# Layer 0's sixth inner product and layer 1's own block sums in a two-layer graph network

## The chip, the core and the metric

The kernel runs on one core of a Trainium2 chip, in one launch. The metric is the device time of that launch in microseconds (us). Before the change it is 2325.86, the median of three runs (2325.35 to 2327.71).

## The reference, cut to what matters

Sixteen batches of N = 1024 nodes with D = 512 features, in float32, share one symmetric 1024 x 1024 adjacency matrix. Two layers follow one another; `layernorm` works over the features.

```python
# layer 0
h = maximum(layernorm(x), 0)
x = x + (einsum('nm,bmd->bnd', adj, h) @ W0 + bias)
# layer 1: graph attention
u  = maximum(layernorm(x), 0)
h  = u @ W1                              # (b, 1024, 512)
s1, s2 = h @ a[:512], h @ a[512:]
e  = leaky_relu(s1[:, :, None] + s2[:, None, :], 0.2) * adj
x  = x + elu(einsum('bij,bjf->bif', softmax(e, axis=2), h) + beta * h)
```

In layer 0 the left matrix of the large product is the same for all batches. In layer 1 it is the batch's own attention matrix.

## The kernel before, in words

**Two phases.** Layer 0 runs for all sixteen batches, then layer 1 for all sixteen. Between them, each batch's residual x1 and its u lie in DRAM. The core's memory is divided into pools of tiles; those that matter here are `b4` (twelve tiles of 512 KB: 128 partitions x 1024 float32), `up` (seven of that size), `xp` (four, residuals), `ld` (two, loads) and `b2` (five of half the size). The eight banks of the matmul engine's result memory (PSUM) are taken from a pool of eight.

**Seven products instead of eight.** Each large product is cut into 2 x 2 blocks and made by the Strassen-Winograd scheme with seven block products, `p1` to `p7` (`PRODUCTS`, L44 to L52). Left operands are the blocks A11, A12, A22 and the sums S1 = A21 + A22, S2 = S1 - A11, S3 = A11 - A21, S4 = A12 - S2; right operands the blocks B11, B21, B22 and the sums T1 = B12 - B11, T2 = B22 - T1, T3 = B22 - B12, T4 = B21 - T2. The order on the matmul engine is p1, p2, p6, p5, p7, p3, p4. Each product has two halves of 128 x 512 results, one PSUM bank each; products that share a letter in `PRODUCTS` accumulate in the same pair of banks (p1, p6, p7 and p4 in Y, p5 and p3 in X, p2 alone in W).

**Reading the banks.** `ReadA` (L121 to L174) takes each finished half out of its bank: p1, p6, p5 and p4 by a copy on ScalarE (to C11, C12, C22, C21), p2 and p7 by an addition on VectorE onto such a copy, p3 by three or four VectorE additions, which make the left operands of the second product. Names in the profile follow: `y` is layer 0's product with the adjacency, `po` its product with W0, `z` layer 1's product with the attention matrix, `pq` its product with W1.

**The inner level.** In layer 0, from the second batch on (`products_a2`, L198 to L311), four of the seven block products, p1, p5, p3 and p4, are cut once more, into seven inner products r1 to r7 of 256-column matmuls (`inner_steps`, L206); p2, p6 and p7 are plain products of eight 512-column matmuls. An inner product needs:

- left sums, three of them and one in place, made per batch on VectorE by `inner_left` (L393), in a tile of `b4`;
- right sums, three of them and one in place, made once in the first batch by `inner_right` (L368) and kept for all of layer 0, in `up`, `b4` and `b2` tiles;
- a scratch tile `t` of `b4`, and combinations: copies on ScalarE after r1, r5 and r7, additions on VectorE after r6, r7 and r3.

The three pairs (p1, p2), (p5, p6), (p3, p7) go in turns: one inner step, one plain step. p4 goes in turns with the first product with the weights.

**Order of the work.** Every engine executes its instructions in the order in which the code issues them (`InOrder`, L103 to L115). The code of a product calls `after(k)` behind each of its steps, and plans map a step k to the helpers that are called there. So the plans decide what stands ahead of what in each engine's queue. In `products_a2` a step is one turn: 0 to 6 for (p1, p2), 7 to 13 for (p5, p6), 14 to 20 for (p3, p7), 21 to 27 for p4. In layer 1, `layer1_a` (L854) has fourteen steps, two per product: step 2n + p is half p of the n-th product, after its bank has been read. `layer1_b` (L869) has fourteen in the same manner for the weighted products.

**What the plans place in layer 0.** `plan_out` (L1083) makes layer 1's u of the *previous* batch from its residual tiles, in place: `stats` (two passes of ScalarE per 128 rows, then the inverse deviation on GpSimd), `relu` (ScalarE), `logits` (VectorE, two reductions per 128 rows, for s1 and s2), `sums` (VectorE, the block sums S1, S2, S4 of u, S3 in place) and `store` (SyncE issues seven stores: four blocks of u, and S1, S2, S4). It also loads the next residual (`load_res`, L548) and calls `inner_left`. The unwanted full result of a `stats` or `logits` pass goes into the tile of S1, which is written later.

**What the plans place in layer 1.** `load_u` (L693) loads the seven tiles of the next batch's u, at the steps in `LOADS_U` (L1170). The softmax of the next batch (`Softmax`, L714) is spread over both parts by `SOFTMAX_A` and `SOFTMAX_B`: row maxima on VectorE, exponentials on ScalarE, transposes on VectorE. Its right sums are made on VectorE: T1 and T2 in the part with W1 (steps 1, 2, 5, 6), T3 at its steps 12 and 13, T4 at steps 6 and 8 of the next batch's `layer1_a`:

```python
SOFTMAX_B = {0: "D", 1: "T1a", 2: "T1b", 4: "d", 5: "T2a", 6: "T2b", 12: "T3a", 13: "T3b"}
LATE_A = {6: "T4a", 8: "T4b"}
```

The u of the last batch is not ready in layer 0. `LateOut` (L663) makes it in pieces during layer 1, and its block sums are made from the loaded blocks by `u_sums` (L701), at steps 10 and 12 of `layer1_b`.

All rows of the profile carry line L111, that of the helper that records each instruction; instructions are told apart by their tiles.

## Time and profile before

| | |
|---|---|
| median of three runs | 2325.86 us |
| the profiled execution: time | 2330.04 us |
| its span (first to last instruction) | 2328.3 us, 28484 instructions |
| matmul engine (PE) busy | 2292.2 us, 98% |
| VectorE (DVE) | 1808.8 us, 78% |
| ScalarE (ACT) | 1503.0 us, 65% |
| GpSimd (POOL) | 586.5 us, 25% |
| DMA | 383.15 MB, mean 165 GB/s |
| clock granted to the matmul engine | 0.996 |
| layer 0, first batch with the set-up | 0 to 89.8 us |
| layer 0, batches 1 to 15 | 89.8 to 1151.9 us |
| layer 1 | 1151.9 us to the end |

Busy time is the sum of an engine's instructions, waits left out. The names of tiles in a row stand as output<-inputs, with numbers of batches left out. Times in a timeline are counted from the start of the span. A bracket at the end of a row gives the idle time before it in us and the instruction whose end closed it.

### The profile page before, as it was taken

What the parts mean: (1) busy time and instruction counts of PE and PEld (TensorE: products, weight loads), DVE (VectorE), ACT (ScalarE), POOL (GpSimd) and SP (SyncE); (2) the same over time, 40 slices, a digit from 0 to 9 for tenths busy, and PEclk for the clock granted to TensorE, in tenths of its full rate; (3) what the DMA queues carried; (4) which work ended last, traced back from release to release, by engine and by line L of the source; (5) the groups of instructions that cost most, each with busy time, mean ns of one, the idle gap of its engine ahead of it and who ended that gap; (6) DMA issues with size and microseconds to landing.
All of it is one profiled execution on the core that took longest, in us unless ns stands there. A gap on an engine that the chain in (4) does not pass through costs nothing.

```text
span 2328.3 us, 28484 instructions
## 1 busy us (share of the span) xinstructions
PE 2292.2 (98%) x7984; PEld 1511.3 (65%) x7984; DVE 1808.8 (78%) x3932; ACT 1503.0 (65%) x4025; POOL 586.5 (25%) x680
## 2 busy tenths in 40 slices
PE   9999999999999999999899999999999999999998
PEld 5777777777777777776655566555665556655565
DVE  7687787888787788787787778777877778777774
ACT  3666667666667566766357667677676776667743
POOL 1333323233323333222101222122220222112220
PEclk9999999999999999999999999999999999999999
DMA  6255443455453455443755546655466554565541
GB/s 212 82 190 179 157 159 129 141 191 182 145 170 114 152 190 164 145 150 108 268 170 164 177 160 200 199 169 193 160 194 197 172 173 151 176 194 156 179 128 42
DMA packets 207247, 383.15 MB, mean 165 GB/s; under 512 B 80240, under 2 KB 88432, under 8 KB 207088
## 3 DMA queue, kind: packets, MB, share of 16 engines
q1 hardware_dynamic: 206768, 380.81, 50.0%
q8 instruction: 63, 1.03, 0.2%
q14 instruction: 96, 0.79, 0.1%
q10 hardware_dynamic: 320, 0.52, 0.1%
HBM read 251.92 MB, written 133.50 MB: 166 GB/s over the span
## 4 chain that ended last, share of the span: by engine, by line
PE 41%; DVE 18%; ACT 17%; DMA 15%; issue 4%; SPq 3%; POOL 3%; DVEq 0%; ACTq 0%; POOLq 0%
PE z_Y L111 8%; PE y_Y L111 6%; PE pq_Y L111 4%; ACT e L111 4%; ACT uS L111 4%; PE po_Y L111 4%; PE z_X L111 4%; DVE e L111 3%; DMA md<-mx 3%; SPq L111 3%; DVE uS L111 3%; DMA x<-in_x_dram 3%; PE z_W L111 2%; DMA mask<-maskd 2%; PE pq_X L111 2%
## 5 line engine op out<-in xcount | busy, mean ns | idle before, releaser
L111 POOL TENSOR_TENSOR x<-x,r 128x512 f32<-128x512 f32 x120 | 226.1, 1895 | 883.8 <-DMA ul_S<-ud_S 398.7
L111 ACT ACTIVATE e<-e,nm 128x256 f32<-128x256 f32 x480 | 237.4, 498 | 168.3 <-DVE nm L111 168.3
L111 DVE CUSTOM_DVE_ANT_0 e<-e,mask 128x256 f32<-128x256 f32 x512 | 239.2, 519 | 73.1 <-DMA mask<-maskd 42.9
L111 POOL TENSOR_TENSOR xr<-xr,bias_bc 128x512 f32<-128x512 f32 x128 | 172.8, 1362 | 231.1 <-DVE xr L111 164.4
L111 PE MATMUL z_Y<-pT,ul_U 128*128 128x512 f32 x512 | 224.9, 592 | 0.0
L111 ACT ACTIVATE e<-s2b,s1b 128x256 f32<-128x256 f32 x512 | 215.1, 507 | 9.2 <-DMA s2b<-s2d 9.2
L111 DVE STREAM_TRANSPOSE pT<-e 128x512 f32<-128x512 f32 x240 | 155.7, 687 | 67.3 <-ACT e L111 67.3
L111 DVE CUSTOM_DVE_ANT_0 uS<-xr,v_bc 128x512 f32<-128x512 f32 x240 | 165.3, 689 | 54.0 <-ACT uS L111 49.4
L111 PE MATMUL po_Y<-w_c,y_C 128*128 128x256 f32 x768 | 192.1, 385 | 7.5 <-DVE xr L111 7.4
L111 PE MATMUL pq_Y<-w_c,z_C 128*128 128x256 f32 x768 | 176.4, 381 | 2.2 <-ACT z L111 1.0
L111 PEld LDWEIGHTS z_Y<-pT,ul_U 128*128 128x128 f32 x512 | 97.3, 190 | 115.6 <-issue 112.2
L111 ACT ACTIVATE r<-z,rs 128x256 f32<-128x256 f32 x192 | 95.7, 499 | 112.1 <-DVE z L111 112.1
L111 PEld LDWEIGHTS po_Y<-w_c,y_C 128*128 128x128 f32 x768 | 147.8, 193 | 30.4 <-DVE xr L111 9.3
L111 PEld LDWEIGHTS pq_Y<-w_c,z_C 128*128 128x128 f32 x768 | 144.6, 190 | 33.4 <-issue 7.7
L111 PE MATMUL y_Y<-adjT_B,h 128*128 128x512 f32 (+1 forms) x332 | 149.7, 554 | 1.4 <-ACT adjT_B L111 1.4
L111 ACT ACTIVATE h<-x,nb_h,r_h 128x512 f32<-128x512 f32 (+1 forms) x132 | 98.1, 792 | 73.8 <-POOL nb_h L111 73.2
L111 ACT ACTIVATE uS<-xr 128x512 f32<-128x512 f32 x120 | 75.4, 629 | 85.2 <-DVE xr L111 65.1
L111 PE MATMUL y_Y<-adjT_T,hS 128*128 128x512 f32 x256 | 128.0, 596 | 0.0
L111 PE MATMUL y_W<-adjT_B,h 128*128 128x512 f32 x256 | 127.2, 592 | 0.0
L111 PE MATMUL po_X<-w_c,y_S 128*128 128x256 f32 x512 | 115.7, 379 | 0.0
L111 PE MATMUL pq_X<-w_c,z_S 128*128 128x256 f32 x512 | 115.6, 379 | 0.0
L111 PE MATMUL z_W<-pT,ul_U 128*128 128x512 f32 x256 | 112.5, 592 | 0.0
(202 smaller groups left out, 4891.3 us busy)
## 6 DMA issues: line engine op xcount, KB each, us to landing
mask<-maskd SPq DMA_DIRECT2D x128, 512.0 KB
x<-in_x_dram SPq DMA_DIRECT2D x64, 512.0 KB
xr<-in_x_dram SPq DMA_DIRECT2D x256, 128.0 KB
x1d<-xr SPq DMA_DIRECT2D x64, 512.0 KB
ul_U<-ud_U SPq DMA_DIRECT2D x64, 512.0 KB
x<-x1d SPq DMA_DIRECT2D x64, 512.0 KB
out_dram<-x SPq DMA_DIRECT2D x252, 128.0 KB
ud_U<-xr SPq DMA_DIRECT2D x60, 512.0 KB
```

The source lines that it names most:

```text
L111: return lambda *args, **kwargs: tc.keep_in_program_order(f(*args, **kwargs))
```

## The change

It has two parts, and a rearrangement around them.

**Inner products.** p2 and p6 become inner products too, so six of seven are. The pairs (p1, p2) and (p5, p6) are now two inner products in turns: r1 of one, r1 of the other, r4, r4, and so on. Where p6 was read in the middle and at the end of its pair, it is now read at the last two turns, beside p5. p3 with p7 and p4 with the weights stay as they were. `INNER` has six entries, the right sums take eight tiles instead of five (seven of `up`, one of `b4`) and the same two of `b2`; `plan_first` makes those of p2 and p6 in the first batch, and `plan_out` and `plan_norm_b` call `inner_left` for p2 and p6 in each.

**Sums of u.** Layer 0 stores only the four blocks of u, each right after its `relu`; `LayerOut.sums` and the three stores of S1, S2, S4 go. Layer 1 loads four blocks and makes the sums with `u_sums`, now in two parts: S1 and S2 (part 0) at steps 10 and 12 of the previous batch's `layer1_b`, S3 and S4 (part 1) at steps 3 and 4 of the batch's own `layer1_a`. For batch 0, part 0 stands at steps -1 and 0 of `layer1_a`. Since the S1 tile that took the unwanted results is no more, there is a tile `junk` of `b4`, which is kept.

**Rearrangement.** `plan_out` has a new order of statistics, normalisations, logits and loads of residuals. In layer 1, T3 moves from steps 12 and 13 of `layer1_b` to steps 5 and 6 of `layer1_a`, and T4 from steps 6 and 8 to 9 and 11.

```diff
-        for two, one in (("p1", "p2"), ("p5", "p6"), ("p3", "p7")):
-            inn, pla = inner_steps(two), plain_steps(one)
-            for m in range(7):
-                inn[m]()
-                pla[m if m < 4 else m + 1]()
-                if m == 0 and two == "p5":
+        for pair in (("p1", "p2"), ("p5", "p6")):
+            turns = list(zip(*(inner_steps(prod) for prod in pair)))
+            for m, turn in enumerate(turns):
+                for step in turn:
+                    step()
+                if m == 0 and k:
                     reads("p2", 0)
                     reads("p2", 1)
-                elif m == 3:
-                    pla[4]()
-                    if one != "p2":
-                        reads(one, 0)
-                elif m == 5:
-                    reads(two, 0)
-                elif m == 6:
-                    for prod in (two,) if one == "p2" else (one, two):
-                        reads(prod, 1)
+                elif m > 4:
+                    for prod in pair:
+                        if prod != "p2":
+                            reads(prod, m - 5)
                 after(k + m)
             k += 7
+        inn, pla = inner_steps("p3"), plain_steps("p7")
+        for m in range(7):
+            inn[m]()
+            pla[m if m < 4 else m + 1]()
+            if m == 3:
+                pla[4]()
+                reads("p7", 0)
+            elif m == 5:
+                reads("p3", 0)
+            elif m == 6:
+                reads("p7", 1)
+                reads("p3", 1)
+            after(k + m)
+        k += 7
...
-    INNER = {"p1": ("A11", "B11"), "p5": ("S1", "T1"), "p3": ("S4", "B22"), "p4": ("A22", "T4")}
+    INNER = {
+        "p1": ("A11", "B11"), "p2": ("A12", "B21"), "p5": ("S1", "T1"), "p6": ("S2", "T2"),
+        "p3": ("S4", "B22"), "p4": ("A22", "T4"),
+    }
...
-                for i, (pl, tag) in enumerate(((up, "up"),) * 4 + ((b4, "b4"),))
+                for i, (pl, tag) in enumerate(((up, "up"),) * 7 + ((b4, "b4"),))
...
+    def junk(k):
+
+        if not junks:
+            junks.append(b4.tile([P, 2, D], F32, tag="b4", name="junk"))
+        return junks[0][:, k, :]
...
-            names = ("U00", "U01", "U10", "U11", "S1", "S2", "S4")
+            names = ("U00", "U01", "U10", "U11")
...
-        def sums(self, q, part):
-            u1, u2 = self.us[0, q], self.us[1, q]
-            left_half(
-                q, u1[:, :, 0:HD], u2[:, :, 0:HD], u1[:, :, HD:D], u2[:, :, HD:D], self.s, (part,)
+        def store(self, nh, q):
+            sp.dma_start(
+                out=ud[self.b][f"U{nh}{q}"], in_=self.us[nh, q].rearrange("p k d -> p (k d)")
             )
...
-    def u_sums(b, q):
+    def u_sums(b, q, part):
         t = uts[b]
+        if q == 0 and part == 0:
+            for n in ("S2", "S1", "S4"):
+                t[n] = up.tile([P, HC, HD], F32, tag="up", name=f"ul_{b}_{n}")
...
             5: [(logit_weights, 0), (logit_weights, 1)], 6: [(w_sums, w0_c)],
...
-            (1, o.stats, 0, 1, 1), (2, o.stats, 1, 0, 0), (3, o.stats, 1, 0, 1),
-            (4, o.relu, 0, 0), (7, o.relu, 0, 1), (8, o.stats, 1, 1, 0), (9, o.stats, 1, 1, 1),
-            (10, o.relu, 1, 0), (11, o.relu, 1, 1),
-            (0, inner_left, b, "p3"), (1, inner_left, b, "p4"), (2, inner_left, b, "p5"),
-            (5, o.logits, 0, 0, 0), (6, o.logits, 0, 0, 1), (8, o.logits, 0, 1, 0),
-            (9, o.logits, 0, 1, 1), (11, o.logits, 1, 0, 0), (12, o.logits, 1, 0, 1),
-            (13, o.sums, 0, 0), (14, o.sums, 0, 1), (14, o.store, 0), (15, o.logits, 1, 1, 0),
-            (16, o.logits, 1, 1, 1), (16, load_res, b, 0, 0), (17, load_res, b, 0, 1),
-            (17, o.sums, 1, 0), (18, o.sums, 1, 1), (18, o.store, 1),
-            (21, load_res, b, 1, 0), (22, load_res, b, 1, 1),
+            (1, o.stats, 1, 0, 0), (2, o.relu, 0, 0), (3, o.stats, 1, 0, 1),
+            (4, o.stats, 0, 1, 1), (7, o.relu, 1, 0), (8, o.relu, 0, 1), (9, o.stats, 1, 1, 0),
+            (10, o.stats, 1, 1, 1), (11, o.relu, 1, 1),
+            (3, o.store, 0, 0), (8, o.store, 1, 0), (9, o.store, 0, 1), (12, o.store, 1, 1),
+            (0, inner_left, b, "p5"), (1, inner_left, b, "p6"),
+            (3, o.logits, 0, 0, 0), (4, o.logits, 0, 0, 1), (8, o.logits, 1, 0, 0),
+            (9, o.logits, 1, 0, 1), (10, o.logits, 0, 1, 0), (11, o.logits, 0, 1, 1),
+            (13, inner_left, b, "p3"), (15, o.logits, 1, 1, 0), (16, o.logits, 1, 1, 1),
+            (16, o.store_logits), (18, inner_left, b, "p4"),
+            (10, load_res, b, 0, 0), (13, load_res, b, 0, 1), (15, load_res, b, 1, 0),
+            (18, load_res, b, 1, 1),
...
-            (10, h_sums, b, 1), (12, inner_left, b, "p1"),
+            (10, h_sums, b, 1), (12, inner_left, b, "p1"), (13, inner_left, b, "p2"),
...
-    SOFTMAX_B = {0: "D", 1: "T1a", 2: "T1b", 4: "d", 5: "T2a", 6: "T2b", 12: "T3a", 13: "T3b"}
+    SOFTMAX_B = {0: "D", 1: "T1a", 2: "T1b", 4: "d", 5: "T2a", 6: "T2b"}
...
-    LATE_A = {6: "T4a", 8: "T4b"}
+    LATE_A = {5: "T3a", 6: "T3b", 9: "T4a", 11: "T4b"}
...
-    LOADS_U = {5: ("U00",), 7: ("U01",), 9: ("U10", "U11"), 11: ("S2",), 13: ("S1", "S4")}
+    LOADS_U = {5: ("U00",), 7: ("U01",), 9: ("U10", "U11")}
...
         plans.append(plan_softmax(LATE_A, sms[b]))
+        plans.append(steps((3, u_sums, b, 0, 1), (4, u_sums, b, 1, 1)))
...
-            plans += [{12: [(w_sums, w1_c)]}, plan_softmax(FIRST_T3, sms[b])]
+            plans += [
+                {12: [(w_sums, w1_c)]}, steps((-1, u_sums, b, 0, 0), (0, u_sums, b, 1, 0)),
+            ]
...
-        if b + 2 == B:
-            plan_b = merged(plan_b, {10: [(u_sums, B - 1, 0)], 12: [(u_sums, B - 1, 1)]})
+        if b + 1 < B:
+            plan_b = merged(plan_b, steps((10, u_sums, b + 1, 0, 0), (12, u_sums, b + 1, 1, 0)))
```

## The prediction

> **What bounds the kernel now.** I read the page first, then who waited for whom on the matmul engine, then the timeline by engine. The page:

> ```profile
> PE 2292.2 (98%) x7984; PEld 1511.3 (65%) x7984; DVE 1808.8 (78%) x3932; ACT 1503.0 (65%) x4025; POOL 586.5 (25%) x680
> ```

> TensorE is the bound: 36 of 2328.3 us are not its own. A change therefore gains what it takes off TensorE and loses every wait that it gives TensorE. What a product costs stands in the timeline of layer 0 (start, us, engine, what, matrix instructions in the row; an f32 matmul counts two):

> ```profile
> 590.46 1.02 PE L111 MATMUL y_Y<-adjT_T,hS 128*128 128x512 f32 x2
> 591.31 1.03 PE L111 MATMUL y_X<-ext,hS 128*128 128x256 f32 x4
> 592.18 1.02 PE L111 MATMUL y_Y<-adjT_T,hS 128*128 128x512 f32 x2
> ```

> From start to start, one 512-column matmul and two 256-column ones both take 0.86. A plain product is 8 x 0.86 = 6.88, an inner one 7 x 0.863 = 6.04: 0.83 less.

> In layer 1, batch 11's adjacency products p7, p3, p4 and the first weighted one stand gapless on TensorE:

> ```profile
> 1983.64 7.03 PE L111 MATMUL z_Y<-pT,ul_U 128*128 128x512 f32 x16
> 1990.50 7.03 PE L111 MATMUL z_X<-pT,ul_S 128*128 128x512 f32 x16
> 1997.37 7.03 PE L111 MATMUL z_Y<-pT_T,ul_U 128*128 128x512 f32 x16
> 2004.24 3.62 PE L111 MATMUL pq_Y<-w_c,z_C 128*128 128x256 f32 x16
> ```

> p4 (1997.37) reads T4; its second half first at 1997.37 + 2 x 0.86 = 1999.1. VectorE in the same stretch:

> ```profile
> 1992.93 1.22 DVE L111 TENSOR_TENSOR pT_T<-pT,pT_T 128x1024 f32<-128x1024 f32 x1
> ...
> 1999.76 0.25 DVE L111 TENSOR_REDUCE nm<-mall 128x16 f32<-128x64 f32 x1
> ...
> 2002.36 1.30 DVE L111 STREAM_TRANSPOSE pT<-e 128x512 f32<-128x512 f32 x2 [2.14 <-ACT e L111]
> 2003.59 0.65 DVE L111 TENSOR_TENSOR z_C<-z_X,z_C 128x512 f32<-128x512 f32 x1
> 2004.27 0.69 DVE L111 TENSOR_TENSOR z_S<-z_C,z_C 128x512 f32<-128x512 f32 x1
> 2005.00 0.69 DVE L111 TENSOR_TENSOR z_S<-z_S,z_C 128x512 f32<-128x512 f32 x1
> 2005.61 0.69 DVE L111 TENSOR_TENSOR z_C<-z_C,z_C 128x512 f32<-128x512 f32 x1
> ```

> The first row is T4's second half, 5 us before its need. The last four are p3's second read: p3 ended on TensorE at 1997.4, and VectorE comes to it only at 2003.6, because the row maximum of the next batch's softmax, ScalarE's exponentials (2.14 waited) and the transposes stand ahead. VectorE runs 6 us late and it costs nothing, as nobody waits for what it does there.

> What a wait costs beyond itself:

> ```profile
> 1138.51 3.62 PE L111 MATMUL po_X<-w_c,y_S 128*128 128x256 f32 x16
> 1146.69 5.41 PE L111 MATMUL po_Y<-w_c,y_C 128*128 128x256 f32 x16 [4.57 <-DVE xr L111]
> ```

> After 4.57 idle, 16 instructions take 5.41 instead of 3.62. The same 5.41 follows an idle 2.29 at 778, and 1.7 us are lost after 2.92 at 1095; nothing after 1.36 at 1122. So I charge 1.8 for each wait over some 2 us.

> [...]

> **The change, part by part.**
> *Matmuls.* p2 and p6 become inner products in 15 batches: 15 x 2 x 0.83 = 24.8 less.
> *Old wait.* Before p5's seventh block (r7) TensorE waits for VectorE 15 times, 8.5 in all. In the changed order VectorE has the two u-sum groups no more and the logits stand elsewhere; walking batch 8, its add is ready at the pair's start + 6.6 and r7 due at + 8.65: gone, -8.5.
> *VectorE in layer 0*, per batch: eight adds for the inner left sums (two groups of 1.46), 1.5 for p2's and 1.9 for p6's combination, less eight u sums at 0.61: +1.4. In batch 0, eight more right sums at 0.69, 5.5 us: y_S is done at 61.6 and due at 69.0, so they hide; uncovered they would cost up to 5. DMAs: three stores and three loads of 512 KB per batch go from SyncE's queue (47 MB of 383); the residual loads stand earlier in it. DMA is half idle; I take nothing, at most -2.
> *ScalarE in layer 0*: six more 256-wide copies, 1.6 to 2 per batch, and this lies on a path. Where p7's first matmul, second in its pair, adds into bank Y0, p6 has just ended there, and now p6's result must first be completed by VectorE and copied by ScalarE (before, p6 was plain, and read half a product earlier). I walk ScalarE's order with its rows, from p1's start: first two copies until 2.2; two statistics passes (1.83 each) 5.9; two copies 6.4; normalisation (two rows, 1.42) 7.8; two passes 11.5; two copies 12.0; C11 twice, with VectorE's adds between, 14.2; two copies 14.7; two normalisations 17.6; two copies 18.1; two passes 21.7; GpSimd's inverse deviation 2.4 (2.58 at 598.06 to 600.64 now); last normalisation 25.6; p5's copy 25.8; VectorE's X0 add, p6's small add, Y0 add 27.4; ScalarE's copy of Y0 28.0. TensorE is there at 24.2 + 0.86 = 25.1. Wait 2.9, from 0 (ScalarE less behind) to 4. Behind it in TensorE's order stands the whole of p7 and p3. With the slow stretch 15 x (2.9 + 1.8) = +70.5.
> *Layer 1, u sums*: 8 x 0.61 = 4.9 more on VectorE per batch (busy 55.7 of 72.2 now). Four stand before a maximum for which it waits 3.09 after waits of 1.30 and 0.84 (batch 11), four among waits of 0.49, 0.96 and 2.13 around the batch's start: hidden; else the batch's chain is late by up to 4.9.
> *T3 and T4.* T3's halves come after steps 5 and 6. Its second stands behind the first transposes (the first maximum comes 26.0 after the batch's start, + 2.6 + 1.25 + 1.15 = 31.0, need at 29.2): a wait of up to 2, which is inside the next. T4's halves move from steps 6 and 8 to 9 and 11. Step 11 is p3's second half, and its four reads are queued first. So T4's second half would end at 2003.59 + 2.62 + 1.15 = 2007.4, need 1999.1. It cannot be earlier than p3's end + 2.62 + 1.15, less 1.72 that TensorE has to do: 2.1, with semaphores 2.3. That is the lower end; the upper is the mean of batches 0 to 14 as they run now: p3's second read starts 48.1 after the batch's start, + 3.8 = 51.9, need 42.9: 9.0. But while TensorE waits, the others catch up: ScalarE's exponents of the layer's end, and by them the next softmax, then start about 2 us earlier against TensorE (bounded by the last weighted product, whose ELU stands ahead of them). I take 7.0. Behind the wait stand p4 and all weighted products. 15 x (7.0 + 1.8) = 132; the last batch has no softmax beside it: 2.4 + 1.8 = 4.2. The periods of layer 1 now sum to 1094.0 for 15 batches against 15 x 72.24: 10.5 of small waits, which the catching up takes away.

> Sum: -24.8 - 8.5 + 70.5 + 132 + 4.2 - 10.5 = +163 on a span of 2328.3, whose execution took 2330.0 against a median of 2325.9; on the median 2489.

> **Rivals.**
> A, the above, 0.70: 2489, own range 2430 to 2545.
> B, only layer 1 waits; ScalarE reaches Y0's copy in time. For it: residual loads come earlier, VectorE's waits of 1.80 and 1.42 for them at 560 may fall away. Against: ScalarE's 25.6 us of work is there anyhow. 2325.9 - 33.3 + 125.7 = 2418; 0.12.
> C, the lag in layer 1 goes: 16 x 2.3 - 10.5 = +26, layer 0 +37, slow stretches 0 to 29: 2389 to 2418; 0.08. Against: the exponentials stand ahead of p3's read in any case.
> D, the other side: ScalarE and VectorE, given time by TensorE's first waits, are never late again. Then layer 0 keeps -33 and layer 1 pays the 2.3 floor without a slow stretch: 2326 - 33 + 26 = 2319. It decides from a layer 1 wait below 2.7 a batch ((33.3 + 10.5)/16). 0.05.
> E, buffers: a scratch tile and one right sum now hold two of the twelve b4 tiles to layer 0's end (one before), and the last batch reloads softmax rows into them: 60 or more on top, over 2545; 0.05. That the inner products are not built is excluded by the built order.

> **How the numbers follow.** Likeliest is A: 2489. The range takes in most of B and C and A's own ends: 2390 to 2545. A run tells 0.2% (5 us) from nothing. Faster: most of D, 0.03; same 0.02; slower 0.95.

> **What the changed profile would show.** TensorE's waits headed by z_Y for VectorE's pT_T, 16 times, 4 to 9 us, and by y_Y for ScalarE's y_C, about 15 times, near 3; y_p5y's wait gone; T4's row right behind four z_ rows; matmuls after each wait at half speed; layer 1 periods near 81 instead of 73. Wrong if these periods stay under 76, or layer 0's fall to 68.

## The result

The changed kernel takes 2468.01 us (median of four runs, 2467.48 to 2472.3), the kernel before 2326.59 on the same chip (2325.35 to 2327.71): a ratio of 1.0612, interval 1.0594 to 1.0630. The forecast was 2489, range 2390 to 2545. TensorE's part of the page after:

```profile
PE 2324.3 (94%) x8344; PEld 1604.4 (65%) x8344; DVE 1909.7 (77%) x4165; ACT 1542.7 (62%) x4115; POOL 546.2 (22%) x680
```

TensorE was left 36 us short of the span before; now it is 146.2 short (2470.5 - 2324.3). Its busy time rose too, by 32 us, although p2 and p6 became cheaper: matmuls at a granted clock of 0.5 are in it (the mean over the span is 0.967, before 0.996). Who made TensorE wait (us in total, times, longest), the head of the list of the kernel before:

```profile
PE y_p5y L111 <- DVE y_p5t L111: 8.5, 15, 2.9
PE po_Y L111 <- DVE xr L111: 7.4, 3, 4.6
PE pq_W L111 <- ACT z_C L111: 3.7, 6, 1.0
```

The same list of the changed kernel, without the set-up:

```profile
PE z_Y L111 <- DVE pT_T L111: 94.3, 16, 7.6
PE y_Y L111 <- ACT y_C L111: 36.7, 15, 3.4
...
PE y_p5y L111 <- DVE y_p5t L111: 1.7, 1, 1.7
```

Both forecast waits head the list, with the forecast counts of 16 and 15. Of the old ones, one of 1.7 is left here and one of 0.6 further down.

The first of them, in batch 11 of layer 1 (starts at 2063.0), the timeline after:

```profile
2101.00 0.69 DVE L111 TENSOR_TENSOR z_C<-z_X,z_C 128x512 f32<-128x512 f32 x1
...
2103.74 0.25 DVE L111 TENSOR_REDUCE nm<-mall 128x16 f32<-128x64 f32 x1
...
2104.24 1.88 PE L111 MATMUL z_Y<-pT_T,ul_U 128*128 128x512 f32 x4
...
2106.34 1.30 DVE L111 STREAM_TRANSPOSE pT<-e 128x512 f32<-128x512 f32 x2 [2.14 <-ACT e L111]
...
2107.57 0.65 DVE L111 TENSOR_TENSOR z_C<-z_X,z_C 128x512 f32<-128x512 f32 x1
2108.26 0.69 DVE L111 TENSOR_TENSOR z_S<-z_C,z_C 128x512 f32<-128x512 f32 x1
2108.98 0.69 DVE L111 TENSOR_TENSOR z_S<-z_S,z_C 128x512 f32<-128x512 f32 x1
2109.59 0.69 DVE L111 TENSOR_TENSOR z_C<-z_C,z_C 128x512 f32<-128x512 f32 x1
2110.19 1.22 DVE L111 TENSOR_TENSOR pT_T<-pT,pT_T 128x1024 f32<-128x1024 f32 x1
...
2111.47 4.71 PE L111 MATMUL z_Y<-pT_T,ul_U 128*128 128x512 f32 x6 [5.35 <-DVE pT_T L111]
```

TensorE begins p4 with T4's first half at 2104.24 and stops after four instructions. T4's second half (2110.19) stands behind p3's second read, that behind the transposes, these behind ScalarE's exponentials, and they behind the maximum at 2103.74, which VectorE reaches as soon as p3's first read (from 2101.00) is done. So even where VectorE lags by nothing, as here, TensorE waits 5.35. The six instructions behind the wait take 4.71, where the four ahead of it took 1.88; the granted clock is 0.50 from 2108.44 to 2115.26.

The other wait, in layer 0, at the end of the pair (p5, p6) of its fifth inner batch, timeline after:

```profile
398.82 1.03 PE L111 MATMUL y_p6y<-adjT_T,hS 128*128 128x256 f32 x4
...
400.58 1.52 ACT L111 ACTIVATE xr<-xr,nb_u,r_u 128x512 f32<-128x512 f32 x2 [1.74 <-POOL nb_u L111]
...
402.00 0.35 ACT L111 COPY y_p5t<-y_p5y 128x256 f32<-128x256 f32 x1
402.26 0.37 ACT L111 COPY y_p6t<-y_p6y 128x256 f32<-128x256 f32 x1
402.39 0.70 DVE L111 TENSOR_TENSOR y_X<-y_X,y_p5t 128x512 f32<-128x512 f32 x1 [2.65 <-ACT y_p5t L111]
...
403.44 0.70 DVE L111 TENSOR_TENSOR y_Y<-y_Y,y_p6t 128x512 f32<-128x512 f32 x1
...
404.18 0.59 ACT L111 COPY y_C<-y_Y 128x512 f32<-128x512 f32 x1 [0.47 <-DVE y_Y L111]
...
404.81 1.74 PE L111 MATMUL y_Y<-adjT_B,h 128*128 128x512 f32 x2 [2.38 <-ACT y_C L111]
```

p5's seventh block is done at 399.0 and p6's at 399.85, but ScalarE stands in u's last normalisation, which itself waited 1.74 for GpSimd's inverse deviation. It copies p5's block only at 402.00; VectorE has idled 2.65 for it; p7's first matmul starts 2.38 late.

Per layer, from the start of each batch's first product: layer 1 begins at 1169.2 instead of 1151.9 (+17.3), and takes 1301.3 instead of 1176.4 (+124.9).

### The profile page after: what moved, and what is told of

The parts are those of the page before. It is cut to its first block, busy times and chain, and to the rows that moved or that the text cites. A ratio compares the mean times of both kernels' runs of the same rounds, so it can differ in the third digit from the quotient of the medians.

```text
span 2470.5 us, 29533 instructions
## 1 busy us (share of the span) xinstructions
PE 2324.3 (94%) x8344; PEld 1604.4 (65%) x8344; DVE 1909.7 (77%) x4165; ACT 1542.7 (62%) x4115; POOL 546.2 (22%) x680
## 4 chain that ended last, share of the span: by engine, by line
PE 27%; DVE 12%; ACT 7%; DMA 5%; SPq 2%; issue 2%; POOL 1%; DVEq 0%; ACTq 0%; POOLq 0%
PE z_Y L111 9%; PE pq_Y L111 8%; ACT e L111 4%; DVE e L111 3%; PE pq_X L111 3%; DMA md<-mx 2%; PE pq_W L111 2%; PE z_X L111 2%; DVE pT L111 2%; PE z_W L111 2%; SPq L111 2%; DVE z_C L111 2%; DMA mask<-maskd 1%; DVE z_S L111 1%; DVE pT_T L111 1%
## 5 line engine op out<-in xcount | busy, mean ns | idle before, releaser
L111 POOL TENSOR_TENSOR x<-x,r 128x512 f32<-128x512 f32 x120 | 209.9, 1762 | 984.9 <-DVE x L111 592.3
L111 ACT ACTIVATE e<-e,nm 128x256 f32<-128x256 f32 x480 | 237.2, 498 | 121.8 <-DVE nm L111 121.8
L111 DVE CUSTOM_DVE_ANT_0 e<-e,mask 128x256 f32<-128x256 f32 x512 | 244.0, 530 | 33.6 <-DMA mask<-maskd 18.1
L111 PE MATMUL z_Y<-pT_T,ul_U 128*128 128x512 f32 x256 | 153.5, 755 | 94.3 <-DVE pT_T L111 94.3
L111 DVE STREAM_TRANSPOSE pT<-e 128x512 f32<-128x512 f32 x240 | 156.3, 689 | 108.3 <-ACT e L111 108.2
L111 PE MATMUL z_Y<-pT,ul_U 128*128 128x512 f32 x512 | 225.2, 592 | 0.0
L111 ACT ACTIVATE e<-s2b,s1b 128x256 f32<-128x256 f32 x512 | 215.0, 504 | 8.7 <-PE po_Y L111 8.7
L111 ACT COPY z_C<-z_Y 128x512 f32<-128x512 f32 x96 | 56.2, 586 | 254.2 <-PE z_Y L111 245.7
L111 POOL TENSOR_TENSOR xr<-xr,bias_bc 128x512 f32<-128x512 f32 x128 | 161.9, 1287 | 222.4 <-DVE xr L111 190.0
L111 PE MATMUL y_Y<-adjT_B,h 128*128 128x512 f32 (+1 forms) x332 | 166.3, 607 | 38.6 <-ACT y_C L111 36.7
L111 PE MATMUL po_Y<-w_c,y_C 128*128 128x256 f32 x768 | 188.3, 379 | 0.0
L111 PEld LDWEIGHTS z_Y<-pT_T,ul_U 128*128 128x128 f32 x256 | 61.5, 248 | 183.6 <-DVE pT_T L111 107.5
L111 DVE CUSTOM_DVE_ANT_0 junk<-xr,v_bc 128x512 f32<-128x512 f32 x240 | 166.4, 693 | 11.1
L111 PE MATMUL pq_Y<-w_c,z_C 128*128 128x256 f32 x768 | 173.7, 379 | 0.0
L111 PEld LDWEIGHTS z_Y<-pT,ul_U 128*128 128x128 f32 x512 | 97.0, 190 | 116.2 <-issue 107.9
L111 PEld LDWEIGHTS pq_Y<-w_c,z_C 128*128 128x128 f32 x768 | 145.8, 190 | 27.1 <-issue 7.7
L111 PEld LDWEIGHTS po_Y<-w_c,y_C 128*128 128x128 f32 x768 | 145.9, 190 | 20.3 <-issue 0.5
L111 ACT ACTIVATE r<-z,rs 128x256 f32<-128x256 f32 x192 | 95.8, 499 | 81.1 <-DVE z L111 81.1
L111 ACT ACTIVATE h<-x,nb_h,r_h 128x512 f32<-128x512 f32 (+1 forms) x132 | 98.2, 793 | 50.2 <-POOL nb_h L111 50.2
L111 ACT ACTIVATE junk<-xr 128x512 f32<-128x512 f32 x120 | 75.9, 632 | 72.6 <-DVE xr L111 70.0
L111 PE MATMUL po_X<-w_c,y_S 128*128 128x256 f32 x512 | 115.7, 379 | 0.0
L111 PE MATMUL pq_X<-w_c,z_S 128*128 128x256 f32 x512 | 115.6, 379 | 0.0
```

The source lines that it names most:

```text
L111: return lambda *args, **kwargs: tc.keep_in_program_order(f(*args, **kwargs))
```

## The experiments

All kernels here compute the whole reference. The kernel before ran at 2328.66, 2331.87, 2331.89 and 2328.39 beside the four groups of runs; ratios are to that.

### Layer 1: T4's place or VectorE's load

Edit of the first (changed kernel, T4 back at its old steps):

```diff
-    LATE_A = {5: "T3a", 6: "T3b", 9: "T4a", 11: "T4b"}
+    LATE_A = {5: "T3a", 6: "T3b T4a", 8: "T4b"}
```

> The changed kernel with T4's halves back at steps 6 and 8 of layer1_a; T3 stays at 5 and 6, u's sums stay in layer 1. Theory A (T4's place): the 16 waits of z_Y for pT_T (94.3 us) go, and with them the slow matmuls behind them (the sixteen periods of layer 1 lose 39 us more than the waits): 2468 - 94 - 40 = 2334, up to 2344 if the small waits of the kernel before come back. Rival R1 (VectorE is overloaded in layer 1 by the 4.9 us of u sums per batch, and T4 is only where that shows): another wait takes its place, periods stay over 76, time over 2390.

Measured: 2335.16, ratio 1.0032 (1.0020 to 1.0044). The wait is gone, with nothing in its place: 14 of the 15 periods of layer 1 (from one batch's first product to the next one's) are 72.24, the time of the matmuls alone, and one is 72.86. Batch 11 (starts at 1962.8) in the timeline of this kernel:

```profile
1996.22 1.21 DVE L111 TENSOR_TENSOR pT_T<-pT,pT_T 128x1024 f32<-128x1024 f32 x1
...
2003.98 7.03 PE L111 MATMUL z_Y<-pT_T,ul_U 128*128 128x512 f32 x16
...
2008.01 0.65 DVE L111 TENSOR_TENSOR z_C<-z_X,z_C 128x512 f32<-128x512 f32 x1
```

p3's second read comes at 2008.01, as late as with the change (45.2 after the batch's start, there 44.6). Nobody waits for it once T4's half stands at 1996.22, ahead of it.

The converse, the kernel before with nothing but T4 moved:

```diff
-    LATE_A = {6: "T4a", 8: "T4b"}
+    LATE_A = {9: "T4a", 11: "T4b"}
```

> The kernel before with one line changed: T4's halves at steps 9 and 11 of layer1_a, as in the change; nothing else of it. Theory A: TensorE waits for T4 in all sixteen batches, 5.4 us or more each and 2.3 in the last, with some 2.6 of slow matmuls behind each, while the small waits of layer 1 (10.5) go: 2326 + 15 x 8.0 + 4 - 10 = 2440, up to 2465 if VectorE lags as in the batches 2 to 9 of the changed kernel (7.0). Rival R1: without the u sums VectorE is in time, so T4's late place costs at most the bare 2.3 a batch without a slow stretch: 2326 + 37 - 10 = 2353 or less.

Measured: 2464.71, ratio 1.0597 (1.0576 to 1.0619). TensorE's waits of this kernel:

```profile
PE z_Y L111 <- DVE pT_T L111: 108.4, 16, 8.5
PE y_p5y L111 <- DVE y_p5t L111: 9.2, 15, 2.2
```

One line, with no sums of u in layer 1 but the last batch's, makes a wait that is even larger than the change's 94.3. Rival R1 falls on both sides: the place alone makes the loss, and the sums don't. The old small waits of the products with W1 (3.7 and 1.5 us in the kernel before) are not in this kernel's list, though its loads are those of the kernel before.

And the smallest mending, the second half one step earlier:

```diff
-    LATE_A = {5: "T3a", 6: "T3b", 9: "T4a", 11: "T4b"}
+    LATE_A = {5: "T3a", 6: "T3b", 9: "T4a", 10: "T4b"}
```

> The changed kernel with only T4's second half moved, from step 11 to step 10, so that it stands ahead of the row maximum and of p3's second read on VectorE, and behind p3's first read. Theory A: with T4 at 6 and 8, p3's first read begins 38.0 after the batch's start (batch 11); + 2.6 + 1.2 = 41.9, and TensorE needs T4's second half at 42.9: in time, with up to 0.6 missing in the most lagging batch. 2335, up to 2342. Rival (VectorE is generally late in the changed layer 1, and each step earlier only gains its own length): the wait shrinks by a step's share, from 5.9 to 2 or more, and the time stays over 2390.

Measured: 2336.57, ratio 1.0018 (1.0011 to 1.0025); the wait for T4 is 0.3, once. It is no gradual matter: between steps 10 and 11 stand the maximum, the exponentials' latency (2.14 in batch 11 above), the transposes and p3's second read, and all of them or none are ahead of T4.

### Layer 0: ScalarE's queue or the structure of the pair

```diff
-            (10, o.stats, 1, 1, 1), (11, o.relu, 1, 1),
-            (3, o.store, 0, 0), (8, o.store, 1, 0), (9, o.store, 0, 1), (12, o.store, 1, 1),
+            (10, o.stats, 1, 1, 1), (13, o.relu, 1, 1),
+            (3, o.store, 0, 0), (8, o.store, 1, 0), (9, o.store, 0, 1), (14, o.store, 1, 1),
```

> The changed kernel with the last normalisation of u in plan_out at step 13 instead of 11 (its store at 14 instead of 12). Theory L0 (ScalarE stands in that normalisation, waiting for GpSimd, while p5's and p6's banks are ready): the copies of p5 and p6 start 3 us earlier, the wait of y_Y for y_C (2.4 a batch, 36.7 in all) falls under 0.5, periods of layer 0 go from 71.64 to about 67.6: 2468 - 15 x 4.0 = 2408. Rival (it is the structure: p6's second bank is only complete at the pair's end, behind p5's sums, whatever ScalarE does): the wait stays over 1.5, time over 2440.

Measured: 2404.60, ratio 1.0340 (1.0315 to 1.0366). Fourteen of the fifteen waits are gone; the last batch keeps its 3.4. Fourteen of the fifteen periods of layer 0 are 67.30 (71.64 with the change), the last is 75.53 in both. The same place of the fifth inner batch, timeline of this kernel:

```profile
381.69 0.37 ACT L111 COPY y_p5t<-y_p5y 128x256 f32<-128x256 f32 x1 [0.18 <-PE y_p5y L111]
...
382.55 0.37 ACT L111 COPY y_p6t<-y_p6y 128x256 f32<-128x256 f32 x1 [0.49 <-PE y_p6y L111]
...
384.15 0.59 ACT L111 COPY y_C<-y_Y 128x512 f32<-128x512 f32 x1 [0.51 <-DVE y_Y L111]
...
384.94 1.02 PE L111 MATMUL y_Y<-adjT_B,h 128*128 128x512 f32 x2
...
385.82 1.52 ACT L111 ACTIVATE xr<-xr,nb_u,r_u 128x512 f32<-128x512 f32 x2
```

ScalarE now waits for TensorE instead of the other way round, and Y0's copy is out at 384.74 for a matmul at 384.94. A margin of 0.2: the structure of the pair, the rival, just fits.

The other half of that question, p2 and p6 plain again (the loop over three pairs of the kernel before, and no left or right sums for p2 and p6):

```diff
-        for pair in (("p1", "p2"), ("p5", "p6")):
-            turns = list(zip(*(inner_steps(prod) for prod in pair)))
...
+        for two, one in (("p1", "p2"), ("p5", "p6"), ("p3", "p7")):
+            inn, pla = inner_steps(two), plain_steps(one)
```

> The changed kernel with p2 and p6 as plain products again, in the order of the kernel before; u's sums, the new order of plan_out and layer 1 as in the change. Theory L0: p6 is read half a product earlier and needs no VectorE sum, so the wait of y_Y for y_C is gone, with the slow stretch: -60; 30 plain products cost 0.83 more each: +25; 2468 - 60 + 25 = 2433, layer 0's periods near 69.3. Rival (the new order of statistics and normalisations is what makes ScalarE late): a wait of 2 or more stays in the pair p5 and p6, now before p5's seventh block or p7: 2468 or more.

Measured: 2428.78, ratio 1.0437 (1.0420 to 1.0453). No wait is left at this place in any batch (one of 1.5, in the last batch, stands at p3's second block); fourteen of the fifteen periods are 68.95. Against 67.30 with the wait mended, two inner products save 1.65 a batch, as forecast (2 x 0.83). The normalisation at step 11 harms only where p6's bank has to be completed behind it.

### Both places mended, and what is left of the change

T4 at steps 6 and 8, and the normalisation at 13:

> The changed kernel with both places mended: T4 at steps 6 and 8, the last normalisation of u at step 13. Theories A and L0 are independent (one in each layer), so the gains add: 2468 - 133 - 63 = 2272. Were they coupled (one wait giving the other its time), it would stay over 2290.

Measured: 2277.40 (2276.74 to 2278.39), ratio 0.9764 (0.9749 to 0.9778). The two causes are independent and their gains add: by the ratios, 1.0612 less 0.0580 for T4's place and 0.0272 for the normalisation's is 0.9760. This version, called the mended kernel below, beats both kernels. TensorE's waits in it:

```profile
PE y_Y L111 <- ACT y_C L111: 3.4, 1, 3.4
PE y_p5y L111 <- DVE y_p5t L111: 1.7, 1, 1.7
```

The rest of the list is in the set-up or under 1. With p2 and p6 plain in it:

> p2 and p6 plain as in the kernel before, T4 at steps 6 and 8; of the change there remain u's sums in layer 1, the six 512 KB transfers a batch fewer, T3's place and the new order of plan_out. From the runs: 2429 - 133 = 2296, so 30 under the kernel before without any inner product. Rival (u's sums and the order of plan_out are worth nothing by themselves, the gain of the mended kernel is that of the inner products): within 5 us of the kernel before.

Measured: 2297.00, ratio 0.9846 (0.9831 to 0.9861). So u's sums in layer 1, with the fewer transfers, T3's place and the order that go with them, are worth 1.5% without the two new inner products; these add 20 us more. Which of the parts brings the 1.5% is not separated here.

### The transfers: what the forecast took as nothing

The loads of S1, S2 and S4 put back in layer 1 of the mended kernel, from another source and overwritten by the sums:

```diff
-    LOADS_U = {5: ("U00",), 7: ("U01",), 9: ("U10", "U11")}
+    LOADS_U = {5: ("U00",), 7: ("U01",), 9: ("U10", "U11"), 11: ("S2",), 13: ("S1", "S4")}
```

> The mended kernel (T4 at 6 and 8, normalisation at 13) with the three 512 KB loads of layer 1 put back, at their old steps 11 and 13: they bring a block of u into the tiles of S1, S2 and S4, which the sums then overwrite; three stores a batch in layer 0 stay away. If the loads cause VectorE's waits for DMA in layer 1 (98.8 us before, 24.6 with T4 back), these return and with them small waits of TensorE: some 10 us more than without, 2282. If the loads are hidden: the same time within 3 us.

Measured: 2281.15 (2277.35 to 2283.73), ratio 0.9778 (0.9763 to 0.9793), between the two expectations. The four times overlap those of the mended kernel, and so do the intervals: the cost of some 4 us is not clear of noise, and the waits have to tell. VectorE's waits for DMA (us in total, times, longest) in the kernel before:

```profile
DVE e L111 <- DMA mask<-maskd: 42.9, 42, 8.1
DVE nm L111 <- DMA mall<-md: 37.9, 26, 3.1
DVE sz L111 <- DMA sall<-sd: 30.5, 14, 3.3
```

In the mended kernel:

```profile
DVE sz L111 <- DMA sall<-sd: 10.1, 11, 2.0
...
DVE nm L111 <- DMA mall<-md: 6.9, 11, 1.5
DVE e L111 <- DMA mask<-maskd: 5.5, 4, 4.2
```

In the mended kernel with the loads:

```profile
DVE sz L111 <- DMA sall<-sd: 35.9, 14, 4.4
...
DVE nm L111 <- DMA mall<-md: 6.9, 13, 1.0
DVE e L111 <- DMA mask<-maskd: 2.6, 4, 1.0
```

111.3 us of waiting became 22.5, which is more than the 4.9 x 15 = 73 of sums that VectorE took over. The loads bring 23 of it back. The layer's fifteen periods exceed 15 x 72.24 by 10.5 before, 0.3 mended, 5.7 with the loads: in these profiled executions they explain about half, and where the waits for masks and maxima went is open.

Then the residual loads of layer 0 at their old steps:

```diff
-            (10, load_res, b, 0, 0), (13, load_res, b, 0, 1), (15, load_res, b, 1, 0),
-            (18, load_res, b, 1, 1),
+            (16, load_res, b, 0, 0), (17, load_res, b, 0, 1), (21, load_res, b, 1, 0),
+            (22, load_res, b, 1, 1),
```

> The mended kernel with the four residual loads of layer 0 back at their old steps 16, 17, 21 and 22 instead of 10, 13, 15 and 18. In the kernel before, GpSimd and VectorE waited 48.2 us, in 30 places, for these loads, and TensorE 7.4 us in three for the residual; in the mended kernel 8.2 in two, and none. If the steps of the loads made the difference: waits of po_Y for xr come back, 5 to 11 us in all with their slow stretches, 2283 to 2288. If it was the three stores that no longer stand ahead of the loads in SyncE's queue: no such wait, the time of the mended kernel (2277) within 3.

Measured: 2282.28 (2280.24 to 2283.06), ratio 0.9779 (0.9762 to 0.9796). The engines wait 49.2 us for residual loads again (8.2 in the mended kernel, 48.2 before), but TensorE has no wait for xr: neither expectation whole. The profiled span is 5.0 longer than the mended kernel's, of which 2.1 lie ahead of layer 1 and 2.2 in the first batch of layer 1, where TensorE waits 2.0 for VectorE. With three stores of a constant tile, to memory that nobody reads, added at step 18:

```diff
+            (18, o.extra),
+        def extra(self):
+            for i in range(3):
+                t = dram.tile([P, 1024], F32, name=f"extra_{self.b}_{i}")
+                sp.dma_start(out=t, in_=adjT["B11"][:, 0:2, :].rearrange("p k d -> p (k d)"))
```

> The mended kernel with the residual loads at their old steps (2282, without a wait of po_Y for xr) and, at step 18 ahead of the last two of them, three more 512 KB stores per batch of a constant tile into memory that nobody reads, as the stores of S1, S2 and S4 stood in SyncE's queue. If those stores, with the loads' steps, made TensorE wait for the residual in the kernel before (7.4 in three places, near 11 with the slow matmuls): po_Y waits for xr return, 2287 to 2293. If not: 2282 within 3, and the cause of that wait stays open.

Measured: 2293.06 (2292.82 to 2296.56), ratio 0.9855 (0.9834 to 0.9875). From the list of TensorE's waits of this kernel:

```profile
PE po_Y L111 <- DVE xr L111: 3.0, 2, 2.8
```

From its view of the tile xr (what the engine waited for ahead of its instructions, us and times):

```profile
  DMA xr<-in_x_dram: 79.8, 42
```

Stores and steps together cost 15.7 by the medians, of which the steps alone are 4.9 (by the ratios 21 and 3.5, as the kernel before was 3.5 quicker beside the last run; the profiled spans differ by 15.1). Of the 15.1, 12.6 lie ahead of layer 1, which begins at 1121.9 instead of 1109.3. TensorE's wait for the residual returns, but it is small here (3.0 of the old 7.4); 2.8 of it stands in the last batch, where the kernel before had its 4.57, and that batch's period is 81.54 (81.97 before, 76.70 mended). The other periods of layer 0 rise by up to 1.3, spread over small lags. Whether it is the stores' place ahead of the last two loads or their traffic that counts is not shown: no run has them behind the loads.

### The last wait

```diff
-        1: "R0", 4: "R1", 7: "B E0 R2", 10: "E1 R3", 12: "R4", 15: "E2", 18: "b R5", 22: "R6",
+        1: "R0", 4: "R1", 7: "B E0 R2", 10: "R3", 12: "R4", 14: "E1", 15: "E2", 18: "b R5", 22: "R6",
```

> The mended kernel with one group of exponentials of layer 1's first softmax moved from step 10 to step 14 of layer 0's last batch, where it stood on ScalarE ahead of p5's and p6's copies: the one wait of y_Y for y_C that is left (3.4, with some 1.9 of slow matmuls) goes, 2277 - 5 = 2272. If VectorE is what is late there: the wait stays over 2, within 2 us of 2277.

Measured: 2277.49 (2276.37 to 2279.31), ratio 0.9762 (0.9747 to 0.9777): no gain over 2277.40. TensorE's waits:

```profile
PE y_p3y L111 <- DVE y_p3t L111: 3.0, 1, 3.0
...
PE y_Y L111 <- ACT y_C L111: 0.9, 1, 0.9
```

The wait fell as forecast, from 3.4 to 0.9, and a new one of 3.0 arose in the next pair, where VectorE's sum for p3 stands behind transposes that wait 1.84 for the moved exponentials. A miss, and the plainest case here of a stall that only changes its place.

## Why the prediction was right

The mechanism of the likeliest case held step by step. Periods of layer 1 are 79.5 to 82.2 (near 81 was forecast, under 76 would have been wrong), those of layer 0 71.64 and in the last batch 75.53 (not 68); in the table all terms are in us of the span. A slow stretch is what a period has beyond its matmuls (67.30 in layer 0, from the run with the normalisation at 13; 72.24 in layer 1) and its waits. The row of the transfers is what the others leave of layer 0's +17.3, so the column sums to the measured difference by construction, but for rounding.

| step of the forecast | forecast | measured |
|---|---|---|
| matmuls of p2 and p6 | -24.8 | 15 x (67.30 - 68.95) = -24.8 |
| old wait at p5 | -8.5 | -6.8 (1.7 is left) |
| layer 0, wait at p7's first matmul | 15 x 2.9 = 43.5 | 36.7 |
| the slow stretch behind it | 15 x 1.8 = 27 | 14 x (71.64 - 67.30 - 2.38) + (75.53 - 67.30 - 3.4 - 1.7) = 30.6 |
| transfers, residual loads and the rest of layer 0 | 0, at most -2 | -18.4 |
| layer 1, wait for T4, 15 batches | 15 x 7.0 = 105 | 94.3 - 2.3 = 92.0 |
| the slow stretch behind it | 15 x 1.8 = 27 | 1214.9 - 1083.6 - 92.0 = 39.3 |
| the last batch | 4.2 | 86.48 - 82.25 = 4.2 |
| small waits of layer 1 | -10.5 | -10.5 |
| sum | +163 | +142.3; the spans differ by 142.2 |

The forecast is 21 high, and the mis-sized terms are these.

*Transfers and the old losses of layer 0.* "DMA is half idle; I take nothing, at most -2" was the wrong price. In the kernel before, the three stores of S1, S2 and S4 stood in SyncE's queue ahead of the batch's last two residual loads, and a DMA busy 50.0% of the span (its main queue, by the page) did not keep TensorE from waiting 7.4 for the residual. The forecast cited 4.57 of that wait, with its release by xr, and left it standing; it also charged 1.8 for each new wait and credited nothing for the half speed behind the old ones. Of the 18.4, 7.4 are that wait, 3.6 the half speed behind two of its three times (5.41 instead of 3.62) and 1.7 that behind the old wait of 2.92 at p5. In the run that puts the stores and the loads' steps back, 12.6 return ahead of layer 1; no run shows what makes the other 5.8.

*Layer 0's wait.* It is 2.38, where 2.9 was taken. The walk through ScalarE's order held: in the fifth inner batch Y0's copy is out 27.5 after p1's start (28.0 was walked), and TensorE stands ready at 25.2 (25.1).

*T4's wait.* It is 6.1 a batch, between 5.35 and 7.6, where 7.0 was taken: the others caught up by 2.7 instead of 2 (p3's second read comes 45.3 after the batch's start in the mean, not 48.1). The lower end of 2.3 was wrong in kind. It put p3's second read right behind p3's end. But the maximum, 2.14 of exponentials' latency and the transposes begin only after p3's first read, so they stand ahead of the second even without lag, and batches 1 and 10 to 14 settle at 5.35. Rival C at its price could therefore not occur, for the reason that the forecast had named against it.

*Slow stretches.* 1.8 came from waits of 2.3 to 4.6; behind waits of 5.35 to 7.6 it is 2.6. The granted clock is half for 6.83 us there in twelve of the fifteen batches, against 3.41 at the waits of layer 0. This error and that on T4's wait cancel by luck: 8.75 a batch against 8.8.

*Small waits of layer 1.* The number held, and its reason is only one of two. They were to go because TensorE's wait lets the others catch up, and the kernel before with T4 late bears that out: it keeps the loads, and its list has none of them. But with T4 back there is no such wait, and they are gone all the same (0.6 is left of 10.5). Fewer loads are part of that, as far as shown.

*T3.* A wait of up to 2 was allowed for and none came: the first maximum stands at 22.1 to 24.2 after the batch's start instead of the mean of 26.0 that was used.

Rival B fell with the 15 waits in layer 0, D with every batch of layer 1, and E with the list of waits, which holds none for a buffer. The uncovered case of u's sums (4.9 a batch) did not arise: mended, layer 1 runs at the pace of its matmuls with the sums in it.

## What to carry to other kernels

Before moving an instruction in an in-order queue, list what stands between the old and the new place, with the latencies that these wait for, and compare the end of that list with the first need: here one step decided over 130 us, and the sums that were added to the engine's load were neither needed for the loss nor enough to make it. Where a product's last bank must pass through two other engines before the next may start, look for long work with a wait of its own just ahead of that passage. And a half idle DMA is no reason to price transfers at nothing (here it was busy 50.0%, and TensorE waited 7.4 us for a residual): look for the engine that waits for them.

## What the hardware showed unexpectedly

The same wait of 2.38 did not always slow what follows. With T4 back, the first inner batch of layer 0, from the timeline of that kernel:

```profile
118.34 1.12 PE L111 MATMUL y_Y<-adjT_B,h 128*128 128x512 f32 x2 [2.38 <-ACT y_C L111]
119.31 1.03 PE L111 MATMUL y_X<-ext,hS 128*128 128x256 f32 x4
```

The second inner batch, same view:

```profile
188.29 1.66 PE L111 MATMUL y_Y<-adjT_B,h 128*128 128x512 f32 x2 [2.38 <-ACT y_C L111]
189.74 1.91 PE L111 MATMUL y_X<-ext,hS 128*128 128x256 f32 x4
191.45 1.38 PE L111 MATMUL y_Y<-adjT_B,h 128*128 128x512 f32 x2
192.66 1.03 PE L111 MATMUL y_p3x<-ext,in_p 128*128 128x256 f32 x4
```

The first runs on at full speed and its batch takes 69.94; the second is slow, and its batch takes 71.63, as do the twelve that follow (71.63 to 71.64).

With T4 back, the half stretch behind the second batch's wait is 3.41 long and begins at 188.75 (the row at 192.66 is at full speed again). In steps of 3.41 counted back from there, the window from 185.34 to 188.75 holds the whole wait (185.91 to 188.29). The first batch's wait (115.96 to 118.34) is cut at 117.07, 21 steps earlier, into 1.1 and 1.3, and no half stretch follows it. In the changed kernel the steps lie elsewhere: there the first batch's wait (115.89 to 118.27) falls into one window (115.06 to 118.47), and all fourteen are slow.

Counted over such windows, in the traces of the kernel before and of the changed one, behind the first 20 us: in the 36 full-speed windows that half the clock followed, TensorE was idle for 2.11 us or more, in the 1305 others for 2.02 or less. Why the clock falls is not shown by this count, and no run moved a wait against the steps on purpose.
